# Second MLP of a macaron block: another order of the last block's products, earlier transposes of the later tokens, three down products kept for the end

## Chip, cores and metric

The kernel runs on one core of one Trainium2 chip. The metric is the device time of one launch in microseconds (us); lower is better. Before the change the median of three runs is 3165.97 us (3165.23 to 3169.49).

## The reference

The input is one sequence of 2048 tokens of width 512 in fp32. It goes through a "macaron" block: half an MLP, attention with 16 heads and a causal mask, and half the same MLP again. The MLP's weights come as 4-bit codes with one scale for each block of 32; the MLP is 4096 wide, and both of its uses share the weights.

```python
gate = jnp.einsum('th,nh->tn', xt, Wg)
up = jnp.einsum('th,nh->tn', xt, Wu)
gelu = jnp.tanh(0.7978845608028654 * (gate + 0.044715 * gate ** 3)) * gate * 0.5 + gate * 0.5
inter = gelu * up
out = jnp.einsum('tn,hn->th', inter, Wd)
...
x = x + 0.5 * _L0_ffn_ref(_layernorm(x, axis=-1), ...)
x = x + _L0_attn_ref(_layernorm(x, axis=-1), ...)
x = x + 0.5 * _L0_ffn_ref(_layernorm(x, axis=-1), ...)
```

## The kernel before

The launch has three stages, one after the other on the time axis of the profile: the first MLP to about 800 us, attention to about 2052 us, and the second MLP (`second_ffn`, from L636) from there to the end. The change touches the last part of attention and the second MLP.

**Products.** The second MLP does its matrix products by Strassen's scheme in Winograd's form, twice over: a block product of 2 x 2 parts takes seven products of sums rather than eight, and each of these is again done by seven. It runs over the tokens in two halves of 1024. In each half there are eight groups g of the MLP's width, two parts h of a group, and seven outer products i for each (the list `problems`, L598, in the order 1, 2, 6, 7, 5, 4, 3). Two neighbours of that list are a *pair*; a half has NP = 56 pairs, so the loop (L1000 to L1039) goes over pairs 0 to 111. With seven products to a block and two to a pair, the seven pairs of a group are the unit of the bookkeeping (`due = n % 7`).

**Inside a pair** (`pair`) the two outer products run side by side: each of seven inner products y is four matmuls of 128x256 (`product`, L737). They fill three PSUM banks, called d, f and e. y=1, 6 and 4 end in a copy by ScalarE (ACT; L754 u1, L767 u2, L776 the last part of o), y=5 in another (L759 u5), and y=2, 7, 3 in an addition by VectorE (DVE) into the result o (L763, L770, L773). As y=6, 7 and 4 reuse the bank d, y=4 can start only when DVE has read y=7 (L770). The order is 1, 5, 2, 6, a, 7, 3, b, 4 where "a" and "b" stand for pieces of another product that are slipped in.

**Recombination.** `recombine(n - 1)` gives three lists of work for the pair before: additions of 128x1024 (L791) run after the second product of the pair (step 1), gelus on ACT (L794) after step 4, and the product with the up part (L803, `inter`, on DVE) after step 6. Of the additions, those for i = 7 and i = 5 are put on GpSimd (POOL), the others on DVE.

**Down.** When a group's seven pairs are done, `down` gives four sums on DVE (L845 to L848) and 14 *pieces* (L866: eight matmuls each, seven products for each half q of the tokens). They are spread over the next seven pairs: 1, 1, 2, 2, 2, 2, 4 of them (`take`, L1024), with one exception at the start of the second half. A piece ends in a multiply-add from PSUM on DVE (L875) or a copy on ACT (L889) and an addition on POOL or DVE (L881), into the residual. Piece products of kind d use one accumulator bank; after the second q, SyncE's queue (SP) reloads the down weights (L831). The tiles `inter` of part h=1 have one buffer for each name, and so has `s`, the down sums.

**Token operands.** The tokens of a half, transposed, stand in b1 (products i = 1 and 2) and b2 (i = 3); `outer_sums` (L616) makes from them the sums ts (i = 5 and 7) and t4 (i = 6), and overwrites part of b2 for i = 4. Its steps are called t3, t2, t4, t1 (L621 to L624). For the inner products, `inner` (L686) makes four sums of each operand: `first` for b1 (its first two steps are `inner_first`, L627), `second` for b2, `third` for ts, `fourth` for t4 (L695, L696, L699 to L702).

**Later tokens.** The tokens of the second half are brought from where they were put aside (`away`), normalized by ACT and transposed by TensorE (PE) while the first half ends: `Later` has load (L662, through SP's queue, three buffers xl), normalize (L941), and transpose (L949 with the copy L950 by ACT). The weights for pair n + 4 are fetched at the end of pair n, also through SP's queue: six transfers, L612 to L614, into a ring of four slots.

**What sets the order.** The order is written out by hand. `at(half, pair, step, ...)` hangs work behind a step of a pair; L957 to L993 list it all. A pair's list runs behind the recombination of the pair before in steps 1, 4 and 6. Each engine takes its instructions in this order, and waits on semaphores.

**The ends.** After the last pair, its additions, gelus, gates and sums and the last group's pieces run (L1006 to L1015). The last steps of attention (L1482 to L1495) hang the layer norm of the next stage behind the last softmax steps by number (`after`), and L1537 to L1546 write out the last projection; half of its pieces go through a spare tile by ACT and are added by POOL (L1144), the rest are added by DVE (L1140).

Of the kernel before, what the change touches and what calls it, by code (L numbers as in the profile page):

```python
# [35 lines left out]
def macaron_kernel(ctx: ExitStack, tc: tile.TileContext, x, packed, scales, wqk, bqk, wv, bv, wo, bo, out):  # L36
# [558 lines left out]
                run(group)  # L595


    problems = [(g, h, i) for g in range(NG) for h in range(2) for i in (1, 2, 6, 7, 5, 4, 3)]  # L598
    NP = len(problems) // 2

    def pair_of(n):
# [34 lines left out]
    def second_ffn(finish, ready, slots):  # L636
# [9 lines left out]
        with tc.tile_pool(name="w2", bufs=1) as wp, tc.tile_pool(name="act2", bufs=1) as ap:  # L646
# [20 lines left out]
            class Tokens:  # L667
# [18 lines left out]
                def inner(self, t):  # L686
# [11 lines left out]
                    return [  # L698
                        lambda: tt(t3, b22, b12, ALU.subtract),  # L699
                        lambda: tt(b12, b12, b11, ALU.subtract),  # L700
                        lambda: tt(t2, t3, b11, ALU.add),
                        lambda: tt(t4, b21, t2, ALU.subtract),  # L702
                    ]
# [79 lines left out]
            def recombine(n):  # L783

                sums, gelus, gated = [], [], []
                half = n // NP
                for g, h, i in pair_of(n):
                    o = {j: outs.get((half, g, h, j)) for j in range(1, 8)}

                    def add(dst, other, eng=nc.vector):  # L790
                        sums.append(lambda: eng.tensor_tensor(dst, dst, other, ALU.add))  # L791

                    def done(row, second, t, g=g, h=h):
                        gelus.append(lambda: nc.scalar.activation(t[:, 0, :], t[:, 0, :], AF.Gelu_apprx_tanh))  # L794

                        def gate():
                            key = half, g, h, second
                            if row == second:
# [4 lines left out]
                            tt(inter[key][:, row, :], t[:, 0, :], t[:, 1, :], ALU.mult)  # L803

                        gated.append(gate)

                    if i == 2:
                        add(o[2], o[1])
                        done(0, 0, o[2])
                    elif i == 6:  # L810
                        add(o[6], o[1])
                    elif i == 7:
                        add(o[7], o[6], nc.gpsimd)
                    elif i == 5:
                        add(o[6], o[5], nc.gpsimd)
                    elif i == 4:
                        add(o[4], o[7])
                        add(o[7], o[5])
                        done(1, 0, o[4])
                        done(1, 1, o[7])  # L820
                    elif i == 3:
                        add(o[3], o[6])
                        done(0, 1, o[3])
                return sums, gelus, gated

# [135 lines left out]
                return lambda: f(*args)  # L961


            first, second, third, fourth = [tokens.inner(t) for t in range(4)]
            for f in first[2:]:
                f()
            at(0, 0, 0, *third[:2])
            at(0, 0, 1, *third[2:])
            at(0, 0, 3, *second[:2])
            at(0, 0, 5, *second[2:])  # L970
            at(0, 1, 1, *fourth)

            for i in range(8):
                at(0, 6 + i, 6, call(later.load, i))
                at(0, 8 + i, 2, call(later.moments, i))
            at(0, 16, 3, later.scales)
            at(0, 53, 5, call(later.load, 0), call(later.load, 1))
            at(0, 53, 6, call(later.normalize, 0))
            where = [(0, 54, 1), (0, 54, 4), (0, 55, 0), (0, 55, 3), (1, 0, 0), (1, 0, 2), (1, 0, 4), (1, 0, 6)]
            for i, place in enumerate(where):  # L980
                at(*place, call(later.transpose, i))
                if i + 2 < 8:
                    at(*place, call(later.load, i + 2))
                if i + 1 < 8:
                    at(*place, call(later.normalize, i + 1))
            t3, t2, t4, t1 = outer_sums(*ready, nc.gpsimd)
            at(0, 55, 5, *first[:2])
            at(0, 55, 6, *first[2:])
            at(1, 0, 6, t3, t2, t4, *third[:3])
            at(1, 1, 0, third[3])  # L990
            at(1, 1, 1, t1)
            at(1, 1, 3, *second)
            at(1, 1, 5, *fourth)  # L993

            fetch(slot(2), pair_of(2))
            fetch(slot(3), pair_of(3))
# [3 lines left out]
            for n in range(2 * NP + 1):  # L1000
                mine = {k: hooks.pop((n, k), []) for k in range(7)}
                sums, gelus, gated = recombine(n - 1) if n else ([], [], [])
                mine[1] = sums + mine[1]
                mine[4] = gelus + mine[4]
                mine[6] = gated + mine[6]
                if n == 2 * NP:  # L1006
                    pieces.pop(0)()
                    for f in mine[1] + mine[4] + mine[6] + down_sums[:2]:
                        f()
                    pieces.pop(0)()  # L1010
                    for f in down_sums[2:]:
                        f()
                    for piece in pieces:
                        piece()
                    break  # L1015
                if n + 4 < 2 * NP:
                    mine[6].append(call(fetch, slot(n + 4), pair_of(n + 4)))
                due = n % 7
                plan = [[], []]
                if pieces:  # L1020
                    for k, f in enumerate(down_sums):
                        if due == (1, 1, 2, 3)[k]:
                            mine[(2, 5, 2, 2)[k]].append(f)
                    take = 0 if n == NP + 1 else (1, 1, 2, 2, 2, 2, 4)[due]  # L1024
                    mid = (take + 1) // 2
                    plan = [pieces[:mid], pieces[mid:take]]
                    del pieces[:take]
                pair(n, tokens, plan if any(plan) else None, mine)
                if n == NP:

                    pieces.pop(0)()
                if n == NP + 6:

                    for q in range(2):
                        residual[q] = res.tile([P, 4, D], F32, tag=f"xq{q}", name=f"xq_second_{q}")
                        nc.sync.dma_start(out=residual[q].rearrange("p t n -> p (t n)"), in_=away[:, q, :])
                if due == 6:
                    assert not pieces
                    down_sums, pieces = down(n // NP, n % NP // 7)  # L1039

    def attention(xT, xT_f, wqk_wv, next_w):
        with tc.tile_pool(name="aw", bufs=1) as aw, tc.tile_pool(name="qk", bufs=1) as qkp, tc.tile_pool(
# [429 lines left out]
            for p in range(NPAIR):  # L1472
# [9 lines left out]
                if p + 1 == NPAIR:  # L1482

                    o2, o3 = project_out(2), project_out(3)
                    fills = [o2[:4], o2[4:8], o2[8:12] + o3[:4], []]
                    for i in range(4):
                        extra.setdefault(STARTS[3] + 1 + 2 * i, []).append(o3[4 + i])
                    for tb in range(2):
                        xT_f.append(x_transposed("f2", tb))
                        norm = Norm(  # L1490
                            "f2", tb, xT_f[tb], lambda nm: an.tile([P, D], F32, tag="xn", name=nm), (), power=True
                        )
                        for i, step in enumerate(norm.steps()):
# [46 lines left out]
            spare = [pp.tile([P, 2, 512], F32, tag="pt", name=f"spare_{i}") for i in range(2)]  # L1540
# [115 lines left out]
```

## Time and profile before

| | us |
|---|---|
| median of three runs | 3165.97 |
| lowest and highest | 3165.23, 3169.49 |
| the profiled execution's own time | 3169.56 |
| its span, first to last instruction | 3167.8 |
| PE busy in the span | 3117.8 (98%) |
| DVE busy | 2050.2 (65%) |
| POOL busy | 1546.1 (49%) |
| ACT busy | 1047.8 (33%) |
| PE busy from 2560 to 3168 us | 587.3 of 608 |
| mean granted clock of PE | 0.994 |

The profiled execution is one launch; its span leaves out 1.8 us around the first and last instruction. In lines of the timeline the first number is the start in us from the start of the span, the second the duration, followed by the engine, the line of the program, the operation, and its output and inputs. A bracket says how long the engine stood idle ahead of it, and what released it. Neighbouring instructions of one kind are joined into one line with a count (x4). PEld is the weight load of PE, which runs beside its matmuls.

### The profile page before, as it was taken

How to read it: one execution, taken by the hardware profiler on the slowest of the kernel's cores; microseconds unless marked ns; L12 is line 12 of the kernel's file. 1: busy time of each engine (PE TensorE's matmuls, PEld its weight loads, DVE VectorE, ACT ScalarE, POOL GpSimd, SP SyncE). 2: the span in 40 equal slices, each digit the busy share in tenths (PEclk: the TensorE clock that was granted, in tenths of full speed). 3: DMA queues.
4: the chain of work that ended last, by engine and by line, in shares of the span. 5: the costliest groups of instructions: out<-in, count | busy, mean ns of one | idle time of the engine just before them, and what ended most of it. 6: DMA issues, size and time to landing. Idle time of an engine off the chain costs nothing. (4 is left out here: it accounts for less than half of the span.)

```text
span 3167.8 us, 45167 instructions
## 1 busy us (share of the span) xinstructions
PE 3117.8 (98%) x16592; PEld 2010.6 (63%) x16592; DVE 2050.2 (65%) x3177; ACT 1047.8 (33%) x2074; POOL 1546.1 (49%) x1534
## 2 busy tenths in 40 slices
PE   7999999999999999999999999999999989999998
PEld 3556565656555575444335434478888878888887
DVE  6666666666665755656564566777667667666775
ACT  5111111111111122355453456543333333333332
POOL 3767574857667562455663467522222223223222
PEclk9999999999999999999999999999999999999999
DMA  4223122212122220000000100064444345444441
GB/s 139 79 84 118 71 94 83 97 60 96 67 90 88 84 78 24 5 14 9 12 9 7 30 21 9 13 196 126 132 127 126 118 123 173 119 123 129 130 122 60
DMA packets 261293, 260.21 MB, mean 82 GB/s; under 512 B 21216, under 2 KB 225616, under 8 KB 257104
## 3 DMA queue, kind: packets, MB, share of 16 engines
q1 hardware_dynamic: 261072, 257.33, 25.2%
q8 instruction: 131, 2.15, 0.3%
q14 instruction: 90, 0.74, 0.1%
HBM read 176.28 MB, written 79.92 MB: 81 GB/s over the span
## 5 line engine op out<-in xcount | busy, mean ns | idle before, releaser
L1373 ACT ACTIVATE pt<-ps 128x512 f32<-128x512 f32 (+3 forms) x608 | 288.2, 529 | 180.2 <-PE ps L1348 117.6
L1188 PE MATMUL pm<-kT,qT 32*128 32x512 f32 (+3 forms) x1280 | 333.0, 574 | 0.0
L1200 DVE TENSOR_REDUCE parts<-pm 128x1 f32<-128x512 f32 x384 | 246.4, 685 | 132.1 <-PE pm L1188 131.7
L737 PE MATMUL d_f<-ys_f,ring 128*128 128x256 f32 x1216 | 322.8, 386 | 8.7 <-DVE o_f L770 6.1
L1397 POOL TENSOR_TENSOR sum<-pt,pt 128x512 f32<-128x512 f32 (+1 forms) x225 | 265.5, 1200 | 91.7 <-ACT pt L1373 89.5
L1348 PE MATMUL ps<-qT,kT 32*128 32x512 f32 (+3 forms) x1280 | 277.8, 535 | 0.0
L737 PEld LDWEIGHTS d_f<-ys_f,ring 128*128 128x128 f32 x1216 | 229.0, 192 | 56.3 <-DVE o_f L770 20.6
L438 PEld LDWEIGHTS po<-wd,inter 128*128 128x128 f32 x1024 | 194.4, 190 | 77.5 <-issue 55.0
L791 DVE TENSOR_TENSOR o_f<-o_f,o_f 128x1024 f32<-128x1024 f32 x128 | 203.6, 1601 | 58.0 <-ACT o_f L776 54.2
L438 PE MATMUL po<-wd,inter 128*128 128x256 f32 x1024 | 241.1, 379 | 0.0
L339 PE MATMUL pg<-xT_f,w 128*128 128x512 f32 x512 | 239.4, 595 | 1.1 <-ACT u L378 1.1
L339 PE MATMUL pu<-xT_f,w 128*128 128x512 f32 x512 | 238.0, 592 | 0.0
L452 POOL TENSOR_TENSOR xq<-xq,d 128x512 f32<-128x512 f32 x124 | 162.4, 1321 | 93.8 <-DVE xq L446 58.0
L881 POOL TENSOR_TENSOR xq<-xq,d_f 128x512 f32<-128x512 f32 x48 | 64.7, 1348 | 293.2 <-DVE xq L875 227.7
L791 POOL TENSOR_TENSOR o_f<-o_f,o_f 128x1024 f32<-128x1024 f32 x48 | 128.7, 2682 | 141.1 <-ACT o_f L776 139.8
L881 POOL TENSOR_TENSOR xq_second<-xq_second,d_f 128x512 f32<-128x512 f32 x45 | 61.4, 1364 | 272.3 <-DVE xq_second L875 217.6
L1260 PE MATMUL av<-pt,vals 128*32 128x256 f32 (+1 forms) x2432 | 190.6, 368 | 2.4 <-ACT both L1282 2.3
L393 POOL TENSOR_TENSOR u<-u,u 128x512 f32<-128x512 f32 x64 | 81.7, 1277 | 208.8 <-ACT u L390 208.8
L438 PEld LDWEIGHTS po<-wd,s 128*128 128x128 f32 x768 | 145.5, 190 | 57.9 <-issue 40.2
L438 PE MATMUL po<-wd,s 128*128 128x256 f32 x768 | 181.4, 379 | 0.0
L339 PE MATMUL pg<-xsum,w 128*128 128x512 f32 x384 | 179.2, 596 | 0.0
L339 PE MATMUL pu<-xsum,w 128*128 128x512 f32 x384 | 177.7, 592 | 0.0
(224 smaller groups left out, 6348.6 us busy)
## 6 DMA issues: line engine op xcount, KB each, us to landing
wd_f<-kept SPq DMA_DIRECT2D x112, 256.0 KB
kept<-wd SPq DMA_DIRECT2D x8, 1792.0 KB
xq<-in_x SPq DMA_DIRECT2D x16, 256.0 KB
pk<-in_gate_codes SPq DMA_DIRECT2D x16, 256.0 KB
sc<-in_gate_scales SPq DMA_DIRECT2D x32, 128.0 KB
pk<-in_up_codes SPq DMA_DIRECT2D x16, 256.0 KB
sc<-in_up_scales SPq DMA_DIRECT2D x32, 128.0 KB
pk<-in_down_codes SPq DMA_DIRECT2D x16, 256.0 KB
```

Of the source, the lines that this page charges most:

```text
L339: nc.tensor.matmul(ps, lhsT=a[:, j, :], rhs=b[:, j, :], start=(j == 0), stop=(j == 1))
L438: nc.tensor.matmul(ps[:, j, :], lhsT=a[i][:, k, bass.ts(2 * q + j, P)], rhs=b[i][:, k, :], start=(k == 0), stop=(k == 1),)
L452: adder.tensor_tensor(dst, dst, other, ALU.add)
L737: nc.tensor.matmul(ps[:, k, :], lhsT=fa[k][y], rhs=fb[k][y], start=first and k == 0, stop=True, skip_group_check=True,)
L791: sums.append(lambda: eng.tensor_tensor(dst, dst, other, ALU.add))
L881: adder.tensor_tensor(dst, dst, other, ALU.add)
L1188: nc.tensor.matmul(ps[a][:, :n], lhsT=q[r, bass.ts(4 * g + i, P)], rhs=k[r, kb * 512 : kb * 512 + n], start=True, stop=True,)
L1200: nc.vector.tensor_reduce(most, scores, AX.X, ALU.max)
L1260: nc.tensor.matmul(dst_, lhsT=lhsT, rhs=rhs, start=kw.get("start", False), stop=True, skip_group_check=True)
L1348: nc.tensor.matmul(ps[a][:, off:], lhsT=k[r, bass.ts(c, P)], rhs=q[r, g * 512 + off : (g + 1) * 512], start=False, stop=True,)
L1373: nc.scalar.activation(pt[:, a, plain[a] :], ps[a][:, plain[a] :], AF.Exp, scale=scale)
L1397: eng.tensor_tensor(s[:, a, off_2:], one[:, a, off_2:], other[:, a, off_2:], ALU.add)
```

## The change

It is all order and placement, in five parts.

1. The products of the last block (g = 7, h = 1) of each half run in the order 1, 2, 6, 5, 3, 7, 4. So the last two pairs hold 5 with 3, and 7 with 4; b1 is read for the last time in pair 53 of the half, and b2 in pair 54 except for the part that product 4 uses. For this block the addition for i = 7 runs on DVE, the one for i = 5 falls away, and i = 3 gets a second addition.
2. The later tokens' loads start at pair 52 with three tiles; transposes 0 to 3 stand in pair 54 and 4 to 7 in pair 55, at every second step, where before they stood in pairs 54, 55 and 56. The sums of the new half move with them: `first` into pair 55, t3 and t2 (now both on DVE) to the first step of pair 56, t4 and `third` (now on POOL) to the next, t1 and `fourth` (POOL) to the start of pair 57. The same sums at the start of the first half move as well: `third` in front of pair 0, on POOL.
3. The exception for pieces at the start of the second half falls away: pair 57 takes one piece, and none runs behind pair 56.
4. The last pair takes one piece rather than four. The three that are left (pof of i = 5, pod of i = 4 and pof of i = 3, for q = 1 of the group before) run after it, between the last pair's additions, gelus and gates.
5. In attention's last steps the norm steps hang one to three places later, and of the last projection's pieces two rather than four go through the spare tile and POOL.

```diff
+    LAST = NG - 1, 1
+        for i in ((1, 2, 6, 5, 3, 7, 4) if (g, h) == LAST else (1, 2, 6, 7, 5, 4, 3))
...
-                    elif i == 7:
-                        add(o[7], o[6], nc.gpsimd)
-                    elif i == 5:
+                        add(o[7], o[6], nc.vector if (g, h) == LAST else nc.gpsimd)
+                    elif i == 5 and (g, h) != LAST:
                         add(o[6], o[5], nc.gpsimd)
...
                         add(o[3], o[6])
+                        if (g, h) == LAST:
+                            add(o[3], o[5])
...
-            first, second, third, fourth = [tokens.inner(t) for t in range(4)]
-            for f in first[2:]:
+            first, second = tokens.inner(0), tokens.inner(1)
+            third, fourth = tokens.inner(2, nc.gpsimd), tokens.inner(3)
+            for f in third + first[2:]:
                 f()
-            at(0, 0, 0, *third[:2])
-            at(0, 0, 1, *third[2:])
-            at(0, 0, 3, *second[:2])
-            at(0, 0, 5, *second[2:])
-            at(0, 1, 1, *fourth)
+            at(0, 0, 1, *second[:2])
+            at(0, 0, 3, *second[2:])
+            at(0, 0, 5, *fourth)
...
-            at(0, 53, 5, call(later.load, 0), call(later.load, 1))
-            at(0, 53, 6, call(later.normalize, 0))
-            where = [(0, 54, 1), (0, 54, 4), (0, 55, 0), (0, 55, 3), (1, 0, 0), (1, 0, 2), (1, 0, 4), (1, 0, 6)]
-            for i, place in enumerate(where):
+            at(0, 52, 5, call(later.load, 0), call(later.load, 1), call(later.load, 2))
+            at(0, 53, 5, call(later.normalize, 0))
+            for i in range(8):
+                place = 0, 54 + i // 4, 2 * (i % 4)
                 at(*place, call(later.transpose, i))
-                if i + 2 < 8:
-                    at(*place, call(later.load, i + 2))
+                if i + 3 < 8:
+                    at(*place, call(later.load, i + 3))
                 if i + 1 < 8:
                     at(*place, call(later.normalize, i + 1))
-            t3, t2, t4, t1 = outer_sums(*ready, nc.gpsimd)
-            at(0, 55, 5, *first[:2])
-            at(0, 55, 6, *first[2:])
-            at(1, 0, 6, t3, t2, t4, *third[:3])
-            at(1, 1, 0, third[3])
-            at(1, 1, 1, t1)
+            t3, t2, t4, _ = outer_sums(*ready, nc.vector)
+            *_, t1 = outer_sums(*ready, nc.gpsimd)
+            at(0, 55, 1, *first[:2])
+            at(0, 55, 3, *first[2:])
+            at(1, 0, 0, t3, t2)
+            at(1, 0, 1, t4, *third)
+            at(1, 1, 0, t1, *tokens.inner(3, nc.gpsimd))
             at(1, 1, 3, *second)
-            at(1, 1, 5, *fourth)
...
                 if n == 2 * NP:
+                    for steps in (mine[1], mine[4]):
+                        old.pop(0)()
+                        for f in steps:
+                            f()
                     pieces.pop(0)()
-                    for f in mine[1] + mine[4] + mine[6] + down_sums[:2]:
+                    for f in mine[6] + down_sums[:2]:
                         f()
+                    old.pop(0)()
                     pieces.pop(0)()
...
-                    take = 0 if n == NP + 1 else (1, 1, 2, 2, 2, 2, 4)[due]
+                    take = 1 if n + 1 == 2 * NP else (1, 1, 2, 2, 2, 2, 4)[due]
...
-                if n == NP:
-                    pieces.pop(0)()
...
-                            after = 2 + i if tb == 0 else (8, 9, 10, 11, 12, 12, 13, 13, 14, 15)[i]
+                            after = ((2, 3, 6, 7, 8, 8, 9, 9, 10, 11), (8, 9, 11, 12, 12, 13, 13, 14, 14, 15))[tb][i]
...
-                if i % 2:
-                    piece(spare[i // 4][:, i // 2 % 2, :])
+                if i in (5, 7):
+                    piece(spare[:, i // 2 % 2, :])
```

More of the change, by code (lines that the diff above doesn't have):

```diff
@@ L595, in ffn @@
                 run(group)
-    problems = [(g, h, i) for g in range(NG) for h in range(2) for i in (1, 2, 6, 7, 5, 4, 3)]
+    LAST = NG - 1, 1
+    problems = [
+        (g, h, i)
+        for g in range(NG)
+        for h in range(2)
+        for i in ((1, 2, 6, 5, 3, 7, 4) if (g, h) == LAST else (1, 2, 6, 7, 5, 4, 3))
+    ]
     NP = len(problems) // 2
@@ L684, in sums, with inner @@
                     return self.operand(x)[:, 0, 256:], t2, t3, t4
-                def inner(self, t):
+                def inner(self, t, eng=nc.vector):
+                    tt = eng.tensor_tensor
                     n = 2 if t < 3 else 1
@@ L797, in gate @@
                             key = half, g, h, second
-                            if row == second:
+                            if key not in inter:
                                 inter[key] = ap.tile(
@@ L1037, in second_ffn @@
                 if due == 6:
-                    assert not pieces
+                    old = pieces
+                    assert len(old) == 3 * (n + 1 == 2 * NP)
                     down_sums, pieces = down(n // NP, n % NP // 7)
@@ L1539, in attention @@
                 step()
-            spare = [pp.tile([P, 2, 512], F32, tag="pt", name=f"spare_{i}") for i in range(2)]
+            spare = pp.tile([P, 2, 512], F32, tag="pt", name="spare")
             for i, piece in enumerate(o2[12:] + o3[8:12]):
-                if i % 2:
-                    piece(spare[i // 4][:, i // 2 % 2, :])
+                if i in (5, 7):
+                    piece(spare[:, i // 2 % 2, :])
                 else:
```

## The prediction, made before the changed kernel ran

> **What bounds the kernel now.** I read the page first, then the engines' busy time in the second MLP, then what TensorE (PE) waited for at its borders, then the timeline there.
>
> ```profile
> PE 3117.8 (98%) x16592; PEld 2010.6 (63%) x16592; DVE 2050.2 (65%) x3177; ACT 1047.8 (33%) x2074; POOL 1546.1 (49%) x1534
> ```
>
> ```profile
> 2560.00:3168.00 608.00, 587.30 (x2670) 509.09 (x2668) 401.71 (x455) 210.21 (x363) 166.81 (x89) 0.98 0.41 121
> ```
>
> PE is the bound. The change removes no matmul (and moves no more bytes), so only PE's idle and half-speed stretches can be won. In the stretch from the change of halves to the end PE is idle 608.0 - 587.3 = 20.7 us. What it waited for at the change of halves (columns: total, times, longest):
>
> ```profile
> PE d_f L737 <- ACT u_f L767: 4.1, 1, 4.1
> PE d_f L737 <- DVE o_f L770: 3.6, 1, 3.6
> PE d_f L737 <- issue: 2.7, 1, 2.7
> PE f_f L737 <- DVE xT_f_sums L700: 1.4, 1, 1.4
> ```
>
> These four are 11.8 us. The timeline says why (start, duration, engine, line, tiles):
>
> ```profile
> 2584.73 0.81 ACT L941 ACTIVATE xl<-xl,nbias,rstd 128x512 f32<-128x512 f32 x1 [4.72 <-DMA xl<-away]
> 2586.06 2.07 PE L737 MATMUL d_f<-xT_f_sums,ring 128*128 128x256 f32 x4 [4.09 <-ACT u_f L767]
> ...
> 2597.23 1.10 PE L737 MATMUL d_f<-xT_f_sums,ring 128*128 128x256 f32 x4 [2.69 <-issue]
> ...
> 2599.77 2.08 PE L737 MATMUL f_f<-xT_f_sums,ring 128*128 128x256 f32 x4 [1.44 <-DVE xT_f_sums L700]
> ...
> 2602.61 3.33 POOL L624 TENSOR_TENSOR xT_f<-xT_f,xT_f 128x1024 f32<-128x1024 f32 x1
> ...
> 2603.65 3.37 DVE L845 TENSOR_TENSOR s_f<-inter_f,inter_f 128x1024 f32<-128x1024 f32 x1
> ...
> 2610.92 1.13 PE L737 MATMUL d_f<-ys_f,ring 128*128 128x256 f32 x4 [3.60 <-DVE o_f L770]
> ```
>
> ACT stands behind a late token load; then token sums are late; then DVE is. A product of four matmuls takes 0.863 us by the distance of starts when warm, but 1.7 to 1.9 in the rows after the first two waits. From 2574.83 to 2610.92 lie 36.1 us for 14 x 0.863 + 4 transposes x 0.47 + 2 pieces x 1.727 = 17.4. So 18.7 are lost: 11.8 idle, some 6.9 at half speed. That is all that the change of halves can give.
>
> The other borders. Attention's tail: PE waits 2.1 for xn_f L149 (until 2022.07), and some 1.5 follow cold. MLP start:
>
> ```profile
> 2056.60 2.07 PE L737 MATMUL d_f<-ys_f,ring 128*128 128x256 f32 x4 [2.66 <-ACT u_f L754]
> ```
>
> The end:
>
> ```profile
> 3137.35 2.04 PE L866 MATMUL poe_f<-wd_f,inter_f 128*128 128x256 f32 x6 [3.26 <-DVE inter_f L803]
> 3140.99 3.75 PE L866 MATMUL pod_f<-wd_f,s_f 128*128 128x256 f32 x8 [1.60 <-issue]
> ```
>
> Here 3.26 + 1.60 idle and 2.0 of slow matmul make 7 us.
>
> **What the Trainium skill says.** (1) "TensorE: Matmul & The Clock Gate", Part 1: the array falls to half its clock after an idle window of about 3.4 us, free-running, and needs as long to come back. The trace agrees on the factor two (0.863 against 1.7 to 1.9); and on a spell of 3 to 6 us, which adds half of its length (the 4.09 idle: slow until 2592, 3 added; the 2.66 at the MLP's start: 1.6). But the product after the 2.69 idle took 1.10 and that after the 3.60 at 2610.92 took 1.13, both warm. So each stall of about 4 us may cost 0 to 3 more. (2) "GPSIMD Engine Reference", 1. Specifications: GpSimd (POOL) shares its SBUF interfaces with VectorE, and they contend where DVE has two SBUF inputs. It agrees: DVE's 128x1024 add takes 1.22 alone and 3.37 beside POOL above, and
>
> ```profile
> 2622.26 4.52 DVE L791 TENSOR_TENSOR o_f<-o_f,o_f 128x1024 f32<-128x1024 f32 x2 [0.78 <-ACT o_f L776]
> 2622.30 3.40 POOL L791 TENSOR_TENSOR o_f<-o_f,o_f 128x1024 f32<-128x1024 f32 x1 [3.94 <-ACT o_f L776]
> ```
>
> two such adds take 4.52. So a POOL add isn't free: it delays DVE by about its own time. (3) "TensorE: Matmul & The Clock Gate", engine queue depths: ACT and DVE are strict FIFOs. It agrees: u_f L767 stood behind the normalize at 2584.73.
>
> **The change part by part**, in the coordinates of the profiled run (3169.56; span 3167.8, so 1.8 outside). That run lies 3.6 above the median 3165.97; I subtract savings from the median.
>
> *Change of halves.* New tokens are transposed in pairs 54 and 55, because the new product order frees b1 after pair 53 and b2 after 54. Eight transposes cost PE the same 8 x 0.47, only earlier. Loads: issue to use took 5.96 (2578.68 to 2584.73) and 4.65 (2564.79 to 2569.44) before; now three buffers are loaded ahead and load i+3 follows transpose i, so it has two transposes' time, about 6.7 us, also past the ring's six DMAs in SP's queue (some 3.3 us). It mostly fits; I allow 0.75 for the first transpose of pair 55. So the 4.09 goes, and with it the 2.69 and 1.44, since the token sums are no longer behind the last transposes. Pair 56 started at 2575.69 with four transposes ahead of it; now all eight are: 2575.69 + 4 x 0.47 + 0.75, near 2578.4. A load that waits for its buffer holds the ring's transfers behind it on SP, but those fill a slot that is used four pairs later, at least 4 x 7 x 0.863 = 24 us: nothing.
> Next late is DVE. At pair 56's first two steps it gets t3 and t2 (before: one of them on POOL), three sums of pair 55 and t4: 6 x 1.14 = 6.84. They can start when y=1 has run and t3's input is copied, about 2579.3, and stand ahead of L763, L770 and L773 in DVE's queue. POOL's four adds of `third` (4 x 1.27) contend; the first falls in between, the second overwrites what t4 reads and waits. So L763 comes at 2579.3 + 6.84 + 1.27 = 2587.4, L770 after two steps of 0.60, and y=4 of pair 56, which needs L770's bank, starts near 2589.2. PE is ready at 2578.4 + 6 x 0.863 + a piece 1.727 = 2585.3: a stall of 3.9.
> Pair 57: PE is ready for its y=4 at 2589.2 + 7 x 0.863 + 1.727 = 2597.0, with a cold spell of 2.8 at 2599.8. POOL's rest of `third`, t1 (2.34) and `fourth` (4 x some 0.8, an estimate from DVE's 0.42 by the ratio 1.27/0.60) meet there DVE's two gates L803, an L791, L845 and the four adds of `second`, all ahead of L770, all with two SBUF inputs: some 8.5 of POOL's time, by half of which DVE's own 7 is stretched. That gives y=4 near 2604, a stall of 4.3, and pair 58 near 2605.5 where it was 2611.89: gain 6. Behind `third` on POOL stand only L881's adds into the residual, for which no matmul waits. Bounds: without contention or cold spells L763 comes at 2586.1 and the first stall is still 2.6; with some 0.9 for the second, pair 58 starts at 2578.4 + 14 x 0.863 + 2 pieces x 1.727 + 3.5 = 2597.4, gain 14.5; with stalls of half as much again, both cold, no gain. The piece that is moved from after pair 56 into pair 57 costs its 1.727 in either place: 0.
>
> *Six moved recombinations.* Each L791 put from POOL (2.35) to DVE (1.14), and the extra add, lie under products; where DVE has room, nothing; without cover, 1.14 each, counted above for pair 56.
>
> *Attention's tail.* Steps of norm 0 and 1 shift by one to three places, so that xn_f no longer holds up the mask behind it. The 2.1 goes, but POOL's rstd, sum, attnT and mask chain ends at 2022.9 as before, and PE resumes at 2023.7 or so: gain 1.5 (0 to 3.6).
>
> *MLP start.* Two spare adds on POOL rather than four (each 1.35) let u1 and so y=6 start 1.5 earlier; DVE takes two L1140 more (2 x 0.65), and `third`, now up front on POOL, contends with the inner sums ahead of L770: y=4 near 2063.2 for 2062.86. Net 0 (-1 to 2.5).
>
> *End.* The last pair loses three pieces (3 x 1.727 = 5.2), so it ends at 3126.7, not 3131.8, and the sums start 5 us sooner; the three pieces fill part of DVE's time. But pod(4) reads an inter buffer that L803 rewrites (one buffer per tag), its L875 must empty PE's accumulator bank before pod(1) can start, and pof(3) reads `s`, which L845 rewrites. I get PE idle about 5 and a cold spell; the third sums-fed piece starts at 3145.3 to 3147.5, before 3146.55. Net 0 (-1 to 1.2).
>
> Sum: 6 + 1.5 + 0 + 0 = 7.5: 3165.97 - 7.5 = 3158.5 (profiled run: some 3162).
>
> **Rivals.** A measurement of this kernel can tell about 0.2% (6.3 us) from no change.
> (a) *The stalls mostly go* (0.25): little contention, no cold spell. 14.5 + 1.5 = 16: 3150. For: the 3.60 stall left no cold spell. Against: the rows of 4.52 and 3.37.
> (b) *DVE takes over as the wait* (0.20): the stalls of pairs 56 and 57 grow to 6 and 8 us, cold at both; 6 more than I count. The change of halves then gives nothing, and only the tail's 1.5 is left: 3164.5. For: DVE is busy 66% in this stretch and gets t3's 1.14 and `third` beside it. Against: DVE has idle time earlier in pair 55, where part of the six adds' work was done before.
> (c) *Slower: the loads are late* (0.10). Loads 3 to 7 each stand ahead of a normalize on ACT, behind which the copies u1, u2 and o stand, for which PE waits. From a landing of 6.7 us each further us costs 5; at 10 us, 5 x 3.3 = 16.5 against the 7.5: 3175. The sides change at 6.7 + 1.5 = 8.2. For: 5.96 was seen, with DMA at 41%. Against: none above 6.
>
> **How the numbers follow.** The forecast has 0.45 (own range 3154 to 3163, from the ends of the cold spells and of the tail's 0 to 3.6), seven tenths of it below 3159.6, the mark of 0.2%. Faster: 0.25 + 0.31 = 0.56; within 0.2%: 0.14 + 0.20 = 0.34; slower: 0.10. The range 3149 to 3168 leaves out (c) and about a third of (a).
>
> **What would show it.** Right: no L941 wait above 1 us on ACT ahead of pairs 54 and 55; pair 56 near 2578; PE's waits there name DVE L763, L770 (their lines shift by 8) rather than ACT; POOL's `third` and DVE's adds at over 1.5 times their length; the end's idle of about 5 before a pod. Wrong: PE waits on transposes or on ACT behind L941 (c); pair 58 before 2600 (a) after 2610 (b); an end that is shorter by over 2 us.

## The result, and the profile after

The changed kernel takes 3169.01 us (median of 12 runs, 3166.84 to 3171.84) where the kernel before took 3165.74 (12 runs, 3162.77 to 3169.49). The ratio is 1.0009, with a 95% interval of 1.0001 to 1.0018. So it is 3.3 us slower, which is below the 0.2% that the prediction took as its mark. The forecast was 3158.5; the time lies above its range of 3149 to 3168. The profiled execution took 3169.86 (span 3168.1).

The page says what the page before said: PE is the bound, and as busy as it was (3116.8 us of the span, before 3117.8).

From 2560 us to the end PE runs 21 matmuls more than before in the same time (2691 for 2670), so something was gained there:

```profile
2560.00:3168.00 608.00, 589.71 (x2691) 511.63 (x2690) 408.79 (x455) 212.94 (x367) 167.24 (x93) 0.99 0.41 122
```

A fixed mark shows where. Each pair ends in one copy on ACT (L776, in the changed kernel L784), so that the starts of these 112 copies time every pair. I add one mark in attention's tail, where the two programs are still the same (a group of `ps` matmuls that starts at 2010.37 before and at 2007.81 after; the 2.6 us by which the profiled runs differ there lie ahead of the change; in the other traces below the mark stands between 2006.80 and 2009.47). The stretches between marks, in us:

| stretch | before | after | difference |
|---|---|---|---|
| mark to the MLP's first product | 41.68 | 47.19 | +5.5 |
| to the copy of pair 1 | 18.45 | 20.21 | +1.8 |
| pair 1 to 53 | 481.07 | 481.06 | 0.0 |
| pair 53 to 58 (change of halves) | 70.02 | 62.21 | -7.8 |
| pair 58 to 110 | 497.43 | 497.60 | +0.2 |
| pair 110 to the end of the span | 48.76 | 51.99 | +3.2 |

The sum is +2.9, which is the measured 3.3 within the spread of the runs. The long stretches agree to 0.2 us, so the change is three separate events: the change of halves gained what was forecast, and a little more; the tail with the start, and the end, lost more than that.

*The change of halves.* PE waits three times there in the changed kernel: 3.62, 3.19, and 0.5 for a normalized tile (before: four waits, 11.8 us). DVE, POOL and PE in pairs 56 and 57:

```profile
2586.96 2.11 POOL L707 TENSOR_TENSOR ys_f<-xT_f_sums 128x512 f32<-128x512 f32 x1 [2.49 <-DVE xT_f_sums L629]
2587.98 2.17 DVE L799 TENSOR_TENSOR o_f<-o_f 128x1024 f32<-128x1024 f32 x1
...
2593.80 2.08 PE L745 MATMUL d_f<-ys_f,ring 128*128 128x256 f32 x4 [3.62 <-DVE o_f L778]
...
2597.34 3.37 DVE L799 TENSOR_TENSOR o_f<-o_f 128x1024 f32<-128x1024 f32 x1
...
2607.07 0.68 DVE L778 TENSOR_TENSOR o_f<-d_f,u_f 128x512 f32<-128x512 f32 x1
...
2607.85 1.10 PE L745 MATMUL d_f<-ys_f,ring 128*128 128x256 f32 x4 [3.19 <-issue]
```

The waits for ACT and for late token sums are gone; y=4 of the pairs 56 and 57 waits for DVE, whose 128x1024 adds (1.22 alone) take 2.17 and 3.37 beside POOL. "issue" in the last line is no cause: the bank that y=4 writes is read by L778, 0.8 us earlier.

*The tail.* The steps of the layer norms move by less than "one to three places": in the first norm five of the ten steps come one or two places later; in the second only the four normalizes do, by one place each, and the transposes stay. Before, DVE made two tiles of the second token block in a row, and PE hardly waited for them:

```profile
2032.72 1.96 DVE L149 TENSOR_SCALAR xn_f<-xq,mv_f,rstd_f 128x512 f32<-128x512 f32 x2 [0.94 <-POOL rstd_f L128]
...
2034.28 1.26 PE L155 MATMUL pt_f<-ident,xn_f 128*128 128x128 f32 x8 [0.18 <-DVE xn_f L149]
```

POOL, DVE, ACT and PE at the same place in the changed kernel:

```profile
2029.11 1.05 POOL L128 TENSOR_TENSOR rstd_f<-rstd_f,expo 128x4 f32<-128x4 f32 x1
...
2030.20 1.49 DVE L149 TENSOR_SCALAR xn_f<-xq,mv_f,rstd_f 128x512 f32<-128x512 f32 x1 [1.25 <-POOL rstd_f L128]
2031.43 2.07 ACT L1387 ACTIVATE pt<-ps 128x512 f32<-128x512 f32 x4 [3.21 <-POOL sum L1411]
2031.74 0.74 PE L155 MATMUL pt_f<-ident,xn_f 128*128 128x128 f32 x4 [1.51 <-DVE xn_f L149]
2033.04 0.69 DVE L1411 TENSOR_TENSOR sum<-pt,pt 128x512 f32<-128x512 f32 x1 [1.36 <-ACT pt L1387]
...
2033.65 1.94 DVE L149 TENSOR_SCALAR xn_f<-xq,mv_f,rstd_f 128x512 f32<-128x512 f32 x2
2035.28 1.10 PE L155 MATMUL pt_f<-ident,xn_f 128*128 128x128 f32 x4 [2.80 <-DVE xn_f L149]
...
2036.72 1.92 PE L1362 MATMUL ps<-qT,kT 32*128 32x512 f32 x8
```

Read it from the bottom: PE waits 2.80 for a normalized tile; DVE made it at 2033.65, because a softmax sum stood ahead of it in its queue, which waited for ACT, which waited for a POOL sum, which stood behind POOL's rstd. Then PE runs cold (the last line took 1.13 before).

*The start.* y=4 of pair 0 waits 3.73 (1.04 before), and the products of pair 1 behind it take 1.9 where a warm one takes 1.03:

```profile
2064.81 2.08 PE L745 MATMUL d_f<-ys_f,ring 128*128 128x256 f32 x4 [3.73 <-DVE o_f L778]
```

*The end.* Behind the last product (3122.94):

```profile
3125.64 1.89 PE L876 MATMUL pod_f<-wd_f,inter_f 128*128 128x256 f32 x8
...
3127.63 0.69 DVE L811 TENSOR_TENSOR inter_f<-o_f 128x512 f32<-128x512 f32 x1 [3.95 <-PE pod_f L876]
...
3131.90 0.68 DVE L885 SCALAR_TENSOR_TENSOR xq_second<-pod_f,xq_second 128x512 f32<-128x512 f32 x1
...
3132.68 3.75 PE L876 MATMUL pod_f<-wd_f,inter_f 128*128 128x256 f32 x8 [5.16 <-issue]
...
3136.23 3.19 PE L876 MATMUL pof_f<-wd_f,s_f 128*128 128x256 f32 x8
```

DVE waits 3.95 for a kept piece, since the gate L811 rewrites the inter tile that the piece reads. Behind that stand three sums and the L885 that empties the accumulator bank, for which PE waits 5.16; then two pieces run cold (3.75 and 3.19 where the warm piece of the first line takes 1.89).

### The profile page after: what moved, and what is told of

It reads as the page before. It is cut to its first block, busy times and chain, and to the rows that moved or that the text cites. A ratio compares the mean times of both kernels' runs of the same rounds, so it can differ in the third digit from the quotient of the medians.

```text
span 3168.1 us, 45173 instructions
## 1 busy us (share of the span) xinstructions
PE 3116.8 (98%) x16592; PEld 2009.2 (63%) x16592; DVE 2056.9 (65%) x3172; ACT 1047.8 (33%) x2072; POOL 1548.7 (49%) x1539
## 4 chain that ended last, share of the span: by engine, by line
PE 93%; DVE 2%; POOL 1%; issue 1%; ACT 1%; DMA 1%; SPq 0%; POOLq 0%; ACTq 0%; DVEq 0%
PE po L438 12%; PE d_f L745 12%; PE pu L339 12%; PE pg L339 12%; PE pod_f L876 7%; PE av L1274 7%; PE pm L1202 6%; PE f_f L745 6%; PE pqk L1113 4%; PE pof_f L876 3%; PE e_f L745 3%; PE ps L1353 2%; PE pv L1130 2%; PE poe_f L876 2%; PE pp L1150 1%; PE ps L1362 1%
## 5 line engine op out<-in xcount | busy, mean ns | idle before, releaser
L891 POOL TENSOR_TENSOR xq<-xq,d_f 128x512 f32<-128x512 f32 x48 | 64.4, 1342 | 300.6 <-DVE xq L885 230.9
L891 POOL TENSOR_TENSOR xq_second<-xq_second,d_f 128x512 f32<-128x512 f32 x45 | 61.5, 1367 | 283.8 <-DVE xq_second L885 220.6
L799 POOL TENSOR_TENSOR o_f<-o_f,o_f 128x1024 f32<-128x1024 f32 x44 | 119.2, 2710 | 135.8 <-ACT o_f L784 134.7
L1274 PEld LDWEIGHTS av<-pt,vals 128*32 128x32 f32 x2432 | 53.0, 108 | 197.8 <-issue 168.1
```

Source lines behind the costliest of these rows:

```text
L1274: nc.tensor.matmul(dst_, lhsT=lhsT, rhs=rhs, start=kw.get("start", False), stop=True, skip_group_check=True)
```

## Experiments

Each kernel differs from the changed kernel or from "the change of halves alone" by the edit shown. Times are medians; those of the kernel before beside them were taken on the same chip. They differ from chip to chip by up to 1.1 us (3165.74 to 3166.80), and a difference between the medians of two experiments is uncertain by as much. Stretches are the ones of the table above.

### 1. The second norm's steps back

```diff
-after = ((2, 3, 6, 7, 8, 8, 9, 9, 10, 11), (8, 9, 11, 12, 12, 13, 13, 14, 14, 15))[tb][i]
+after = ((2, 3, 6, 7, 8, 8, 9, 9, 10, 11), (8, 9, 10, 11, 12, 12, 13, 13, 14, 15))[tb][i]
```

> The changed kernel, with only the second norm's steps (tb = 1) of attention's tail put back to 8, 9, 10, 11, 12, 12, 13, 13, 14, 15. Theory: the losses of the changed kernel come from three separate places; the tail's is that xn_f stands in DVE's queue behind a softmax sum (PE waits of 1.5 and 2.8 on L149, then cold matmuls), because each normalize now stands only a step ahead of its transpose. Then these waits go, the MLP starts about 4.9 us earlier, and the time is 4 to 5 below the changed kernel's (3169.0), about 3164.5. Rival: the stall only shows up in the tail because DVE and POOL are full there; with the old steps PE waits for them elsewhere, and the time stays within 1.5 us of the changed kernel's.

3164.85 (before 3166.39; ratio 0.9994, 0.9986 to 1.0003), so some 4.2 below the changed kernel. From the mark to the MLP 42.28 rather than 47.19: 4.9, as expected. With both normalizes ahead of the softmax sum in DVE's queue, all eight transposes run in one piece:

```profile
2029.35 1.94 DVE L149 TENSOR_SCALAR xn_f<-xq,mv_f,rstd_f 128x512 f32<-128x512 f32 x2 [1.25 <-POOL rstd_f L128]
...
2030.89 1.27 PE L155 MATMUL pt_f<-ident,xn_f 128*128 128x128 f32 x8 [1.51 <-DVE xn_f L149]
```

So 4.9 of the tail's 5.5 us are this one step's delay of the second block's normalizes. Some 0.4 of the rest are the two spare pieces that DVE adds in place of POOL (experiment 10).

### 2. The MLP's start back

`third`, `second` and `fourth` of the first half on DVE at their old places, and four spare pieces:

```diff
-            for f in third + first[2:]:
+            for f in first[2:]:
...
+            at(0, 0, 0, *third[:2])
+            at(0, 0, 1, *third[2:])
...
-                if i in (5, 7):
+                if i % 2:
```

> The changed kernel, with the MLP's start as before: the sums third, second, fourth on DVE in the pairs 0 and 1, and four spare pieces on POOL. Theory: in the changed kernel y=4 of pair 0 waits 3.7 because POOL's third and DVE's second run against each other, and the clock falls; with the start as before the wait is some 2.7 + 1.0 in two parts and one cold spell less, so the time falls by 1.5 to 2.5, to about 3167. Rival: DVE's work up to L778 takes as long either way (8.3 us in both traces), so that nothing changes (within 0.7 us).

3166.79 (before 3166.39; ratio 1.0003, 0.9995 to 1.0011). Mark to copy of pair 1: 64.43 for 67.40, 3.0 less. The loss does come from the start; the size is a little above what was expected, and the start of the kernel before itself took 17.30 to 18.48 us to the copy of pair 1 in six traces (20.21 to 20.40 in three traces of the changed one). The edit puts back the place of the sums on POOL and that of `second` in DVE's queue together, so which of the two made the wait is not separated. This run also showed something at the change of halves, where its program is that of the changed kernel. Its lines there:

```profile
2592.51 2.08 PE L745 MATMUL d_f<-ys_f,ring 128*128 128x256 f32 x4 [3.62 <-DVE o_f L778]
...
2605.79 0.68 DVE L778 TENSOR_TENSOR o_f<-d_f,u_f 128x512 f32<-128x512 f32 x1
...
2606.57 2.04 PE L745 MATMUL d_f<-ys_f,ring 128*128 128x256 f32 x4 [4.61 <-issue]
```

From y=4 of pair 56 to L778 of pair 57 it is 13.28 us, in the changed kernel 13.27. But here PE came out of its cold spell earlier in pair 57, reached the wait earlier, waited 4.61 rather than 3.19, and went cold again (2.04 for 1.10). The stretch became 65.15 for 62.21: a PE that was faster for a while lost 2.9 us.

### 3. The end back

The last pair takes four pieces, and none is kept.

```diff
-                    take = 1 if n + 1 == 2 * NP else (1, 1, 2, 2, 2, 2, 4)[due]
+                    take = (1, 1, 2, 2, 2, 2, 4)[due]
...
```

> The changed kernel, with the end as before: the last pair takes four pieces and none is kept. Theory: the kept pieces cost 3.2 us at the end, since DVE waits for one of them (L811 at 3127.6), and PE then for DVE (5.2) and runs cold; so the time falls by 3 to 3.5, to 3165.7. Rival: the order of the last block's products is what makes the end slower (three sums of the last pair rather than the ones of before), not the kept pieces: then the time stays within 1 us of the changed kernel's or rises.

3166.67 (before 3166.39; ratio 1.0000, 0.9992 to 1.0008), 2.3 below the changed kernel, and by the trace 48.88 from pair 110 to the end where the changed kernel has 51.99: 3.1. The order of the last block alone costs nothing that can be seen (before: 48.76; the old end took 46.96 to 49.12 in six traces).

### 4. The change of halves alone

Parts 1 to 3, with the tail, the start and the end of the kernel before: the edits of 2 and 3, and both norms back.

```diff
-after = ((2, 3, 6, 7, 8, 8, 9, 9, 10, 11), (8, 9, 11, 12, 12, 13, 13, 14, 14, 15))[tb][i]
+after = 2 + i if tb == 0 else (8, 9, 10, 11, 12, 12, 13, 13, 14, 15)[i]
```

> The kernel before with the order of products, the later tokens' transposes and the sums at the change of halves alone (parts 1 to 3), so the changed kernel without the tail, the start and the kept pieces. Theory: the parts add up; the change of halves gains 7.9 us (pairs 53 to 57 by the distance of their copies in the two traces), so 3165.7 - 7.9 = 3157.9. Rival: the gain at the change of halves stands on the late start (a shifted phase of the DMA or a warmer clock), or is given back at the end by the last block's order: 3162 or more.

3161.24 (21 runs, 3156.95 to 3165.53; before 3166.39; ratio 0.9985, 0.9978 to 0.9991). So 5.2 us faster, between the two cases. The profiled run has 65.22 in the stretch from pair 53 to 58, as in experiment 2: PE fell cold behind the wait in pair 57. What is lost is neither a gain given back at the end (47.81 there) nor the DMA (PE waits 0.5 for a late normalize, as in the changed kernel); by this trace it is the clock after this one wait.

The rival is not ruled out, though. Seven traces have the same program from pair 53 to 58. The stretch is 62.2 us in the three that have the changed kernel's start (the changed kernel, experiments 1 and 3), and 64.5 to 65.3 in the four that have another (2, 4, 5 and 7). So of the 7.8 us, some 3 may go with the start; why they should was not tested.

### 5. Another end

Two pieces kept, not three; the one that reads the inter tile (i = 4) runs inside the last pair.

```diff
-                orders = [...] if final else [DOWN, (1, 2, 6, 7, 5, 4, 3)]
+                orders = [...] if final else [DOWN, DOWN if (half, g) == (1, NG - 2) else (1, 2, 6, 7, 5, 4, 3)]
...
-                    take = 1 if n + 1 == 2 * NP else (1, 1, 2, 2, 2, 2, 4)[due]
+                    take = 2 if n + 1 == 2 * NP else (1, 1, 2, 2, 2, 2, 4)[due]
...
-                    old.pop(0)()
```

> The change of halves as in the changed kernel (tail and start as before), with another end: the last pair takes two pieces (7 and 4, in the order 1, 2, 6, 7, 4, 5, 3), two are kept (5 and 3) and run right behind the last product; the sums stand between them in DVE's queue. Theory: what costs at the changed kernel's end is not that pieces are kept but that one of them (pod of i = 4) reads the single inter buffer that the gate of pair 110 rewrites, and that DVE stands behind it with all of the last pair's sums. With it inside the pair DVE starts its sums about 2 us after the last product, and 3.5 us of PE's work lie beside them: from the last copy but one (pair 110) to the end some 44 us, where the kernel before has 48.8, the changed one 52.0 and the change of halves alone 47.8. Rival: the end is a chain of DVE, which the kept pieces don't shorten, and PE goes cold in any case: 47 us or more.

3157.58 (before 3166.80; ratio 0.9972, 0.9961 to 0.9984). From pair 110 to the end 46.61, and 44.94, 44.94 and 46.63 in the three later kernels with the same end (9 to 11): 44 was not reached, but all lie below the old end (46.96 to 49.12 in six traces) and the changed kernel's (50.47 to 51.99 in three). By the two traces the end accounts for 1.2 of the 3.7 us by which the median is below experiment 4; the same end differs by 1.7 from trace to trace. That two pieces are kept and not three, and that the one with i = 4 runs inside the pair, are changed together here. What is left is DVE, with POOL beside it:

```profile
3125.66 2.35 DVE L811 TENSOR_TENSOR inter_f<-o_f 128x512 f32<-128x512 f32 x2
...
3130.51 3.26 PE L876 MATMUL pod_f<-wd_f,s_f 128*128 128x256 f32 x8 [2.56 <-issue]
```

Two gates take 2.35, where two take 1.28 without a POOL add (L891) beside them, and PE waits 2.56 for the sums that follow.

### 6. `second` behind y=3

```diff
-            at(1, 1, 3, *second)
+            at(1, 1, 5, *second)
```

> The change of halves alone (as in x4_halves_only), and in it the four sums of `second` two steps later in pair 57, behind y=3 (step 5 for 3). Theory: the last wait at the change of halves (PE for L778 in pair 57, 3.2 to 4.6 us) is DVE's queue: in two traces 13.28 and 13.27 us lie between y=4 of pair 56 and L778 of pair 57 whatever PE's clock did, and 4.1 of them are these four sums. With them behind L778 the copies of pairs 53 and 58 stand 59 us apart, where it was 62.2 (PE warm) and 65.2 (PE cold behind the wait). Rival: the wait only moves, to y=5 of pair 58, which needs two of the sums, or stays with POOL's sums: 61.5 or more.

3154.85 (5 runs, 3153.63 to 3155.12; before 3166.80; ratio 0.9961, 0.9949 to 0.9974). The stretch is 60.01 us, and the wait in pair 57 is 0.45 rather than 3.1 to 6.0 (the seven traces of experiment 4):

```profile
2595.64 0.67 DVE L778 TENSOR_TENSOR o_f<-d_f,u_f 128x512 f32<-128x512 f32 x1
...
2596.41 1.10 PE L745 MATMUL d_f<-ys_f,ring 128*128 128x256 f32 x4 [0.45 <-POOL ys_f L709]
```

The wait was the order of DVE's queue. In all seven traces without this edit 13.26 to 13.29 us lie between y=4 of pair 56 and L778 of pair 57, whether PE was warm or cold in between. A smaller wait took its place: y=5 of pair 58 waits 1.14 for a sum of `second`, which is why it is 60.0 and not 59.

### 7. Another start

The first norm as in the changed kernel, the second as before; two spare pieces; `third` on DVE in pair 0; `second` and `fourth` only in pair 1. Against the change of halves alone:

```diff
-            at(0, 0, 3, *second[:2])
-            at(0, 0, 5, *second[2:])
-            at(0, 1, 1, *fourth)
+            at(0, 1, 1, *second[:2])
+            at(0, 1, 3, *second[2:])
+            at(0, 1, 5, *fourth)
...
-                            after = 2 + i if tb == 0 else (8, 9, 10, 11, 12, 12, 13, 13, 14, 15)[i]
+                            after = ((2, 3, 6, 7, 8, 8, 9, 9, 10, 11), (8, 9, 10, 11, 12, 12, 13, 13, 14, 15))[tb][i]
...
-                if i % 2:
+                if i in (5, 7):
```

> The change of halves alone, and three edits of the tail and the start: the first norm's steps (tb = 0) as in the changed kernel, the second's as before; two spare pieces rather than four, as in the changed kernel; `third` on DVE in pair 0 as before, but `second` and `fourth` first in pair 1. Theory: the first norm's new places are good for 1.3 us, two spare pieces free y=6 of pair 0 from the wait on u1 (2.7 us), and what made the changed kernel slow there was the second norm and POOL's sums against DVE's. From the softmax product at 2010.37 (before) to the copy of pair 1 it was 60.1, in the changed kernel 67.4; now 54 to 56. Rival: the ten additions on DVE at the end of attention (L1154) make DVE late for pair 0 whatever else is done: 59 or more.

3158.83 (before 3166.80; ratio 0.9971, 0.9961 to 0.9981). Mark to the copy of pair 1: 57.06 (before 60.12), 1.1 us above what was expected, with 14.8 after the MLP's first product (before 18.45). The first norm's new steps give nothing, though: 42.29 from the mark to the MLP, and 42.09 in experiment 9 with the old steps. With the new ones the wait of 2.1 of the kernel before is gone, and two others stand in its place:

```profile
PE pt_f L155 <- DVE xn_f L149: 1.5, 1, 1.5
PE av L1270 <- ACT pt L1385: 1.2, 1, 1.2
```

At the change of halves this trace is the counterpart of experiment 2. PE stayed warm behind the wait of pair 56, so it was early in pair 57, waited 6.02 there, and only then went cold; the stretch is 64.50:

```profile
2583.50 1.13 PE L745 MATMUL d_f<-ys_f,ring 128*128 128x256 f32 x4 [3.62 <-DVE o_f L778]
...
2597.56 2.04 PE L745 MATMUL d_f<-ys_f,ring 128*128 128x256 f32 x4 [6.02 <-issue]
```

### 8. All sums of the new tokens on DVE

As 6; t4 and `third` behind y=3 of pair 56, t1 and `fourth` behind y=7 of pair 57, none on POOL.

```diff
-            at(1, 0, 1, t4, *tokens.inner(2, nc.gpsimd))
+            at(1, 0, 5, t4, *third)
-            at(1, 1, 0, t1, *tokens.inner(3, nc.gpsimd))
+            at(1, 1, 4, outer_sums(*ready, nc.vector)[3], *fourth)
```

> As x6_second_late, with all sums of the second half's tokens on DVE: t4 and `third` behind y=3 of pair 56, t1 and `fourth` behind y=7 of pair 57, nothing of them on POOL. Theory of the shared port: POOL's help is worth nothing where DVE adds from SBUF at the same time, since each delays the other by about its own time; with the sums also behind L771 and L778 in pair 56, the copies of pairs 53 and 58 stand no further apart than in x6_second_late, and rather 1 to 2 us closer. Rival: POOL does take work off DVE; the 5.2 us of sums (third 2.4, t1 1.1, fourth 1.7) that DVE gets here make it 2 to 5 us longer than x6_second_late.

3156.58 (before 3166.80; ratio 0.9968, 0.9955 to 0.9980); the stretch is 61.16, 1.1 more than in 6. Neither case came, but the theory is half right. In pair 56 the sums of the pair before run unstretched (1.22 and 1.23), and the wait is 1.54 for 3.62; of these 2.1 some 1.2 are t4 (an add of 1.22), which now stands behind L778. From DVE's first sum, L628, to L778 of pair 57 it takes 16.7 us, where 6 takes 19.0 with four sums fewer (DVE shows no idle time in between in either trace):

```profile
2578.39 1.23 DVE L799 TENSOR_TENSOR o_f<-o_f 128x1024 f32<-128x1024 f32 x1
...
2582.13 1.13 PE L745 MATMUL d_f<-ys_f,ring 128*128 128x256 f32 x4 [1.54 <-DVE o_f L778]
...
2591.05 0.68 DVE L778 TENSOR_TENSOR o_f<-d_f,u_f 128x512 f32<-128x512 f32 x1
```

Up to there POOL's help was worth less than nothing. It is lost behind: t1 and `fourth` stand ahead of the sums that y=5 of pair 58 needs, PE waits 2.42 and goes cold.

### 9 to 11. The parts together

The change of halves with the edit of 6, the start of 7 with both norms as before, and the end of 5 (the edits are shown there):

> The best of the parts together: the change of halves with `second` behind y=3 of pair 57; both norms of the tail as before; two spare pieces on POOL, `third` on DVE in pair 0, `second` and `fourth` first in pair 1; the end with two kept pieces (5 and 3). Theory: the parts add up by their places. Tail as in the kernel before plus 0.3 to 0.6 for two spare pieces less on POOL (41.5 to 42.3 from the mark to the MLP's start), 14.8 to the copy of pair 1, 60 at the change of halves, 46.6 at the end: 3150 to 3152, which is 15 us below before. Rival: each gain so far rests partly on where the clock's window fell, and together they give no more than the best of them alone (3154.9).

3152.12 (5 runs, 3151.27 to 3152.59; before 3166.72; ratio 0.9955, 0.9941 to 0.9968), 14.6 us faster than before. The stretches are 42.09, 14.77, 481.08, 60.32, 497.43 and 44.94. The parts add up.

The same with four spare pieces on POOL (`if i % 2`):

> As x9_all, but with four spare pieces on POOL as before. Theory: the wait for u1 in pair 0 (2.7 us, and a cold spell after it) comes from these two more additions on POOL, so the stretch from the MLP's start to the copy of pair 1 is 2.5 to 4 us longer than in x9_all, and the attention's tail at most 0.6 shorter. Rival: since DVE must do the two additions in x9_all, the stretch is the same within 1 us.

3153.97 (ratio 0.9958, 0.9946 to 0.9971). From the MLP's first product to the copy of pair 1 it is 18.39 rather than 14.77, and the tail is 0.37 shorter: the wait for u1 (2.7) and the cold products after it came from the two more POOL additions.

The same as 9, with `third` of the second half on DVE (`at(1, 0, 5, t4, *third)`):

> As x9_all, with t4 and `third` of the second half on DVE behind y=3 of pair 56, and t1 and `fourth` on POOL as in x9_all. Theory of the shared port: in x8_dve_only DVE reached L778 of pair 57 16.7 us after its first sum (L628), where it took 19.0 in x6_second_late with `third` on POOL, although it had four sums more; x8 lost this again because t1 and `fourth` stood ahead of L781. With these on POOL the copies of pairs 53 and 58 stand 58 to 59 us apart (x6_second_late 60.0, x8_dve_only 61.2). Rival: POOL's sums now meet DVE's in pair 57 in full, and it is 60 or more.

3151.03 (ratio 0.9954, 0.9941 to 0.9966), not to be told from 9. The stretch is 60.72: the expectation missed. With `third` off its queue POOL came to t1 earlier, and stretched a sum of pair 55 instead; the wait in pair 56 stayed (3.70):

```profile
2574.97 3.39 POOL L631 TENSOR_TENSOR xT_f<-xT_f,xT_f 128x1024 f32<-128x1024 f32 x1 [1.16 <-DVE xT_f_sums L628]
...
2576.07 3.38 DVE L799 TENSOR_TENSOR o_f<-o_f,o_f 128x1024 f32<-128x1024 f32 x1
```

## Why the prediction was wrong

**Change of halves: right in mechanism, and in part lucky in size.** To compare, take 4.71 off the changed kernel's times, by which pair 53 is late. Pair 56 was forecast at 2578.4; it started at 2583.11 - 4.71 = 2578.4. Its y=4 was put at 2589.2 with a stall of 3.9: 2589.1 and 3.62. That of pair 57 at 2604 with 4.3: 2603.1 and 3.19. The gain was 7.8 for 6; with other starts of the MLP the same program gained 4.8 to 5.5 (experiments 2, 4, 5 and 7), because PE went cold behind the second wait. The shared SBUF interface of the Trainium skill's "GPSIMD Engine Reference", 1. Specifications, was the right thing to price (adds of 1.22 took 2.17 and 3.37), and rival (c), late loads, came to 0.5 us.

**Attention's tail: the failed step.** "The 2.1 goes [...] gain 1.5 (0 to 3.6)": measured, 5.5 were lost. I looked at the wait that the change takes away, and not at what each moved step now stands behind. The second norm's steps were moved too, and I gave them no price: one step later every normalize but the first tile's stands behind a softmax sum in DVE's queue. Experiment 1 puts that at 4.9 of the 5.5. Even the first norm's part is worth nothing (experiments 7 and 9): behind the wait of 2.1 stood others of 1.2 and 1.5. The rule of the forecast itself, to ask who is queued behind whom, was used for the change of halves and not for the second norm; and the range had no case with a loss in the tail.

**MLP start: right in place, wrong in size.** The forecast compared the starts of y=4 alone. y=4 of pair 0 came 9.8 after the MLP's first product rather than the 11.1 forecast (before 10.8), as u1 came earlier. But it ran into one wait of 3.73 rather than two of 2.66 and 1.04, and pair 1 ran cold behind it: +1.8 where 0 (-1 to 2.5 of gain) was said. The term that was missing is the cold spell behind the wait.

**End: the stall right, its price wrong.** The forecast had PE idle for some 5 us before a pod; it was 5.16, for the reason given. It said net 0; it was 3.2. The two pieces after it took 3.75 and 3.19 rather than 1.89 each, 3.1 us in all from start to start, and waits of 0.9 and 1.0 followed. The third sums-fed piece, forecast at 3145.3 to 3147.5, came at 3149.8 (3146.86, and 2.94 added by which the copy of pair 110 was early). I had allowed for "a cold spell", and put its middle at nothing.

So 6 + 1.5 + 0 + 0 should have been 7.8 - 5.5 - 1.8 - 3.2 (and -0.2 by a wait in between). That the sum came close to nothing is chance; no step of the rival for "no gain" (b) took place.

What stays open is what decides whether a wait leaves PE cold. In the seven traces of experiment 4 PE waited 3.62 in pair 56. It was warm behind it in experiment 7, cold for some 3 us in 2, 4 and 5, and cold for some 6 us in the changed kernel and in 1 and 3. In pair 57 waits of 3.1 to 3.2 left it warm, and waits of 4.5 to 6.0 cold. That it is a matter of where the wait falls in a free-running window, as "TensorE: Matmul & The Clock Gate" (Part 1) says, agrees with this, but no run here shifted the phase on purpose. The idle time of about 3.4 us that the page names is no threshold here: the wait of 2.66 at the MLP's start before left PE cold too (2.07 for 1.03).

## What to carry to other kernels

For every step that a change moves, also one on an engine with idle time, look up what stands ahead of it in its queue at the new place and follow that chain to its end; a normalize that was one step late cost 4.9 us through four engines. A stall of PE cost its length and up to some 3 us more of half speed behind it. Where PE waited for the order of DVE's queue, moving work behind the instruction that frees PE's bank was the cheapest cure (experiment 6: one digit, 5.2 us less in the stretch than with the cold wait). Work given to GpSimd beside a busy VectorE was not free: in experiment 8 VectorE reached the same instruction 2.3 us sooner with four sums more of its own and none on GpSimd.

## What the runs showed of the hardware

A PE that gets warm earlier can lose: in experiment 2 it reached the same DVE instruction 1.4 us earlier, waited that much longer, and the colder clock after it cost 2.9 us. In experiment 7 it stayed warm, waited 6.02, and lost 2.3.

The runs of one kernel spread with the clock. In the 21 runs of the change of halves alone the five with a mean granted clock of 0.998 took 3156.95 to 3159.43 us, and the two with 0.994 took 3164.69 and 3165.53. The spread is 8.6 us there, and 1.5 us in five runs of the same with the wait of pair 57 taken away (experiment 6). That this wait is the reason is argued, not shown: experiment 11, where it is 1.4, still spread over 4.6 us in five runs.
